# Latent attention and ternary gated experts: query weights in four held transfers, two transposes in accumulator banks

## The chip, the cores and the metric

The kernel runs on one core of one Trainium2 chip. The metric is the device time of one execution in microseconds, the lower the better. The core has TensorE (PE: matrix products and transposes into PSUM banks), VectorE (DVE), ScalarE (ACT), GpSimd (POOL) and SyncE (SP), whose queue issues every transfer between the chip's memory and the on-chip memory. The engines run side by side and wait for one another by semaphores.

## The reference

The input is a batch of 2 sequences of 2048 rows of 512 numbers, 4096 rows in all. Two layers follow one another, each with a layer norm ahead, a layer norm behind and a residual addition:

```python
Q = (hidden_states @ Wq.T + bq).reshape(b, t, H, HD).transpose(0, 2, 1, 3)
V = (hidden_states @ Wv.T + bv).reshape(b, t, H, HD).transpose(0, 2, 1, 3)
attn_logits = jnp.einsum('bhtd,lhd->bhtl', Q, latent) / math.sqrt(HD)
topk_logits, topk_idx = jax.lax.top_k(attn_logits, K_TOP)
attn_weights = jax.nn.softmax(topk_logits, axis=-1)
weighted = jnp.einsum('bhtk,bhtkd->bhtd', attn_weights, selected)
attn_output = (weighted + V).transpose(0, 2, 1, 3).reshape(b, t, d)
return attn_output @ Wo.T + bo
...
scale = jnp.mean(jnp.abs(w)) + EPS
q = jnp.clip(jnp.round(w / scale), -1.0, 1.0) * scale
hidden = jax.nn.silu(up) * gate
return jnp.einsum('bse,de->bsd', hidden, wd)
...
x = x + _layernorm(_L0_attn_ref(_layernorm(x, axis=-1), ...))
x = x + _layernorm(_L0_ffn_ref(_layernorm(x, axis=-1), ...))
```

There are 16 heads of 32 numbers, 64 latent keys for each head, of which a row keeps the best 4, and 2048 hidden units in the experts, whose three weight matrices are reduced to the signs -1, 0 and 1 times one scale each.

## The kernel before

The 4096 rows are worked in 8 blocks of 512 rows, a block in 4 tiles of 128 rows. For a block, the attention part normalizes the rows, brings them into the transposed form (512 features on the partitions), projects queries (4 chunks `c` of 128 features, each a sum over 4 pieces `k` of the query weights), forms the logits with the latent keys, finds the best four on VectorE, and projects values and output. The expert part then runs over 16 chunks of 128 hidden units. In the steady state the attention of one block is woven into the expert loop of the block before.

The change lies in the start, ahead of the first expert loop. There the order of the work on all engines is the hand-written list `FIRST_STEPS`: each word is a step, looked up in the dictionary `STEPS`, with its numbers as arguments, and every engine carries out its instructions in the order in which the steps issue them. The words that matter here are:

- `ast t`: `a_stats` of tile t of the first block, two VectorE instructions (L249, L250).
- `ars lo_hi`: `a_rstd`, the reciprocal root for the tiles lo to hi - 1, two GpSimd instructions (L256, L257). The first one covers two tiles, the others one each.
- `aap t`: `a_apply`, the normalization of tile t on VectorE (L276).
- `atr t`: `a_trans_pe`, four TensorE transposes of a tile into one PSUM bank (L286). The bank comes from `at_psum`, a pool of two buffers that everything short-lived uses.
- `acp t`: `a_copy`, the copy of that bank into the transposed rows `hT`, on ScalarE (L571) but for tile 3, which VectorE copies (L569).
- `q c`, `qc c`: the four products of query chunk c (L577) in a bank of `acc_psum`, a pool of four buffers, and its copy with the bias on ScalarE (L592). The first needs all four tiles of `hT`.
- `hold`: `hold_weights`, which writes one column of the latent keys' tile `lk` on VectorE (L853) and then issues the transfers of `load_weights` on SyncE. The transfer of `lk` has to wait for that write, and in SyncE's order all later ones stay behind it.
- `bh`, `bl`: preparation of the output bias, on ScalarE and VectorE; `nst`: statistics of the second block; `l`, `lc`: logits and their copy (L602, L610); `m`, `r`, `e`, `n`: the best four and the softmax (VectorE and ScalarE, L385 to L413); `s` with u, g or d and a number: the sum of absolute values of one piece of up, gate or down weights on ScalarE (L206); `totg`: the total over the gate pieces on TensorE (L214).

Ahead of the list SyncE issues the four row tiles of the first block (`load_x(0)`, L134) and the query weights as a single transfer of 1 MB (L161). TensorE meanwhile runs 16 products of a matrix of ones (L187), whose results nobody reads; each is two passes in the trace. `load_weights` then issues the latent keys, the biases, the value weights (1 MB), the latent values, the output bias, the second block's rows, and the up, gate, output and down weights in a fixed order. Transfers use eight semaphores in turn, so a transfer is issued only when the eighth before it has landed.

Of the kernel before, what the change touches and what calls it, by code (L numbers as in the profile page):

```python
# [17 lines left out]
P = 128  # L18
# [14 lines left out]


FIRST_STEPS = """
ast0 hold ast1 ars0_2 ast2 ars2_3 ast3 ars3_4 aap0 aap1 atr0 aap2 atr1 acp0 aap3 atr2 acp1 atr3 acp2 acp3 q0 bh
q1 qc0 bl nst0 l0 nst3 qc1 su0 nst1 v0 lc0 nst2 lc1 nrs su2 m1 su3 m0 l1 su1 r0 q2 lc2 su5 nap0
e0 r1 su6 ntr0 qc2 q3 ncp0 nap3 su7 nap1 nap2 sg1 n0 sg2 ob0 ob1 m2 ob2 e1 v1 qc3 n1 lc3 sg4 r2
t0 t1 tc0 ob3 tc1 sg5 m3 ntr2 e2 ntr1 ncp2 r3 y0 ncp1 l2 yc0 sg7 o3_0 n2 e3 o2_0 sd0 n3 v3 lc5
# [19 lines left out]
def latent_attention_ternary_glu(  # L59
# [15 lines left out]
    nc = tc.nc  # L75
    NT, D = x_in.shape
    E = wuT.shape[1]
    DC = D // P
# [18 lines left out]
    def at_psum(name):  # L97
        return ps_at.tile([P, 512], F32, tag="at", name=name)
# [11 lines left out]
    def transposed(which, b, name, dtype):  # L110
        return work.tile([P, DC, TB], dtype, tag=f"{which}{b % 2}", name=name, bufs=1)
# [17 lines left out]
    def load_x(b):  # L129
        x_tiles[b] = []  # L130
        for t in range(TT):
            xt = work.tile([P, D], F32, tag="x", name=f"x_{b}_{t}", bufs=2 * TT)
            r = b * TB + t * P
            nc.sync.dma_start(out=xt, in_=x_in[r : r + P, :])  # L134
            x_tiles[b].append(xt)
# [10 lines left out]
    def load_up(n, src, pieces):  # L146
        for i in pieces:
            k, h = halves[i]
            nc.sync.dma_start(
                out=raw[n, i], in_=src[k * P : (k + 1) * P, h * CH : (h + 1) * CH]  # L150
            )

    load_x(0)
    wq = wpool.tile([P, DC, D], F32, name="wq")
# [3 lines left out]
    bo_sb = wpool.tile([P, D], F32, name="bo_sb")  # L158
    lk = wpool.tile([P, DC, 2 * L], F32, name="lk")
    lv = wpool.tile([P, H // 2, HP], F32, name="lv")  # L160
    nc.sync.dma_start(out=wq, in_=wqT.rearrange("(c p) n -> p c n", p=P))  # L161

    def load_weights():
        nc.sync.dma_start(out=lk, in_=latk)
        nc.sync.dma_start(out=bqv_sb, in_=bqv)
        nc.sync.dma_start(out=wv, in_=wvT.rearrange("(c p) n -> p c n", p=P))
        nc.sync.dma_start(out=lv, in_=latv)
        nc.sync.dma_start(out=bo_sb, in_=bo.to_broadcast([P, D]))
        load_x(1)
        load_up("u", wuT, (0, 2, 3, 1, 5, 6, 7, 4))  # L170
        load_up("g", wgT, (1, 2, 4, 5))
        nc.sync.dma_start(out=wo, in_=woT.rearrange("(c p) n -> p c n", p=P))
        load_up("g", wgT, (7, 6, 0, 3))
        for i in (0, 2, 3, 6, 7, 9, 8, 1, 5, 4):
            rows = 2 * P if i < 6 else P
            r = i * 2 * P if i < 6 else 12 * P + (i - 6) * P
            nc.sync.dma_start(
                out=raw["d", i].rearrange("p (c n) -> p c n", n=D),
                in_=wdT[r : r + rows, :].rearrange("(c p) n -> p c n", p=P),
            )  # L180
# [2 lines left out]
    both = work.tile([P, 2, P], F32, tag="hid", name="ones", bufs=2)  # L183
    ones = both[:, 0, :]
    nc.vector.memset(ones, 1.0)
    for i in range(16):
        nc.tensor.matmul(at_psum(f"ones_{i}")[:, :P], lhsT=ones, rhs=ones, start=True, stop=True)  # L187
    ident = wpool.tile([P, P], F32, name="ident")
    make_identity(nc, ident)
# [93 lines left out]
    def transpose_row(h, name, psum=at_psum):  # L283
        pt = psum(f"pt_{name}")
        for c in range(DC):
            nc.tensor.transpose(pt[:, c * P : (c + 1) * P], h[:, c * P : (c + 1) * P], ident)  # L286
        return pt.rearrange("p (c k) -> p c k", k=P)
# [252 lines left out]
    class FirstAttention(Attention):  # L540
# [19 lines left out]
        def a_trans_pe(self, t):  # L560
            if self.hT is None:
                self.hT = transposed("X", self.b, f"hT_{self.b}", F32)
            self.pt = getattr(self, "pt", {})
            self.pt[t] = transpose_row(self.rows.pop(("a", t)), f"a{self.b}_{t}")

        def a_copy(self, t):
            dst, src = self.hT[:, :, t * P : (t + 1) * P], self.pt.pop(t)
            if self.b == 0 and t == 3:
                nc.vector.tensor_copy(dst, src)  # L569
            else:  # L570
                nc.scalar.copy(dst, src)  # L571
# [277 lines left out]
        return work.tile([P, TB], F32, tag=tag, name=f"qT_0_{c}", bufs=2)  # L849


    def hold_weights():
        nc.vector.memset(lk[:, 0, 0:1], 0.0)  # L853
        load_weights()

    STEPS = {
        "ast": A.a_stats,
# [6 lines left out]
        "l": A.l_pe,  # L864
        "lc": A.l_copy,
        "hold": hold_weights,
        "m": A.m,
        "r": A.r,
# [296 lines left out]
```

## Time and profile before

| what | us |
|---|---|
| median of 4 runs | 1142.31 |
| lowest and highest run | 1141.56, 1142.65 |
| the profiled execution, its own time | 1142.39 |
| its span, first to last instruction | 1140.6 |
| VectorE busy in it | 835.6 |
| ScalarE busy in it | 412.5 |
| the query weights' transfer: issue at, time to landing | 2.57, 7.9 |
| a piece of up weights (512 KB), issue to landing, median of 8 | 8.0 |
| TensorE waiting for rows of tile 0 (L286) | 0.80 |

Times within the profile count from the first instruction. A line of an instruction group gives the line of the kernel, the engine, the operation, the tile written and the tiles read, their shapes, how often it ran, how long it was busy, and the idle time of its engine just before it with the instruction or transfer that ended it. Products on TensorE overlap, so two of them lie closer together than one is long. "Issue to landing" of a transfer contains the time in which it stands behind others.

### The profile page before, as it was taken

What the parts mean: (1) busy time and instruction counts of PE and PEld (TensorE: products, weight loads), DVE (VectorE), ACT (ScalarE), POOL (GpSimd) and SP (SyncE); (2) the same over time, 40 slices, a digit from 0 to 9 for tenths busy, and PEclk for the clock granted to TensorE, in tenths of its full rate; (3) what the DMA queues carried; (4) which work ended last, traced back from release to release, by engine and by line L of the source; (5) the groups of instructions that cost most, each with busy time, mean ns of one, the idle gap of its engine ahead of it and who ended that gap; (6) DMA issues with size and microseconds to landing.
All of it is one profiled execution on the core that took longest, in us unless ns stands there. A gap on an engine that the chain in (4) does not pass through costs nothing.

```text
span 1140.6 us, 14491 instructions
## 1 busy us (share of the span) xinstructions
PE 1127.6 (99%) x4602; PEld 771.7 (68%) x4602; DVE 835.6 (73%) x2952; ACT 412.5 (36%) x715; POOL 164.7 (14%) x204
## 2 busy tenths in 40 slices
PE   8999999999999999999999999999999999999997
PEld 5547666767667665766667766586675866758885
DVE  6978968687866887678877778678786787846435
ACT  4985542332233332333214333153322433224223
POOL 1057003110032000320002200022001120020100
PEclk9999999999999999999999999999999999999999
DMA  9800221432213322222222223242321412102001
GB/s 346 309 0 22 72 93 42 107 120 84 85 50 97 102 87 79 73 76 93 93 74 75 83 93 97 61 102 64 117 71 56 111 65 93 63 3 74 37 1 37
DMA packets 98572, 97.16 MB, mean 85 GB/s; under 512 B 8384, under 2 KB 71104, under 8 KB 98496
## 3 DMA queue, kind: packets, MB, share of 16 engines
q1 hardware_dynamic: 98496, 96.24, 27.2%
q8 instruction: 36, 0.59, 0.2%
q14 instruction: 40, 0.33, 0.1%
HBM read 59.51 MB, written 36.70 MB: 84 GB/s over the span
## 4 chain that ended last, share of the span: by engine, by line
PE 87%; DMA 6%; DVE 5%; ACT 1%; issue 0%; SPq 0%; DVEq 0%; ACTq 0%
PE pg L716 19%; PE pu L716 19%; PE acc L759 18%; PE po L468 8%; PE pv L440 8%; PE pq L353 7%; PE pv L457 2%; PE pl L367 2%; DMA hT<-far_a 2%; DMA raw_d<-in_wdT 1%; DVE left L393 1%; DMA raw_g<-in_wgT 1%; DMA wv<-in_wvT 1%; DVE m L385 1%; PE pq L577 1%; DMA raw_u<-in_wuT 1%
## 5 line engine op out<-in xcount | busy, mean ns | idle before, releaser
L716 PE MATMUL pg<-hT_f,tern_g 128*128 128x512 f32 x512 | 207.8, 406 | 0.0
L716 PE MATMUL pu<-hT_f,tern_u 128*128 128x512 f32 x512 | 204.9, 401 | 0.0
L759 PE MATMUL acc<-tern_d,hi 128*128 128x512 f32 x512 | 203.6, 398 | 0.0
L759 PE MATMUL acc<-tern_d,lo 128*128 128x512 f32 x512 | 200.0, 391 | 1.0 <-DVE lo L749 0.8
L716 PE MATMUL pg<-lT_f,tern_g 128*128 128x512 f32 x512 | 199.8, 390 | 0.0
L716 PE MATMUL pu<-lT_f,tern_u 128*128 128x512 f32 x512 | 199.1, 390 | 0.0
L725 ACT ACTIVATE h<-pu,columns 128x512 f32<-128x512 f32 x128 | 87.1, 681 | 203.0 <-PE pu L716 203.0
L728 DVE SCALAR_TENSOR_TENSOR h<-h,pu 128x512 f32<-128x512 f32 x128 | 85.9, 671 | 94.1 <-ACT h L725 94.1
L744 ACT CAST hi<-h 128x512 fp32r<-128x512 f32 x128 | 79.1, 618 | 199.0 <-DVE h L733 199.0
L733 DVE TENSOR_TENSOR h<-h,pg 128x512 f32<-128x512 f32 x128 | 86.5, 676 | 63.4 <-PE pg L716 62.2
L759 PEld LDWEIGHTS acc<-tern_d,hi 128*128 128x128 f32 x512 | 96.1, 188 | 32.9 <-issue 13.6
L716 PEld LDWEIGHTS pg<-hT_f,tern_g 128*128 128x128 f32 x512 | 96.1, 188 | 25.3 <-issue 1.4
L716 PEld LDWEIGHTS pu<-hT_f,tern_u 128*128 128x128 f32 x512 | 96.0, 188 | 25.2 <-issue 3.1
L759 PEld LDWEIGHTS acc<-tern_d,lo 128*128 128x128 f32 x512 | 96.2, 188 | 22.8 <-DVE lo L749 2.2
L716 PEld LDWEIGHTS pu<-lT_f,tern_u 128*128 128x128 f32 x512 | 96.2, 188 | 22.5 <-issue 3.1
L716 PEld LDWEIGHTS pg<-lT_f,tern_g 128*128 128x128 f32 x512 | 96.3, 188 | 21.5 <-issue 2.9
L749 DVE TENSOR_TENSOR lo<-h,hi 128x512 fp32r<-128x512 f32 x128 | 89.8, 702 | 23.2 <-ACT hi L744 23.2
L440 PE MATMUL pv<-hT,wv 128*128 128x512 f32 x224 | 100.7, 593 | 0.4 <-ACT w L375 0.4
L393 DVE MATCH_REPLACE8 left<-m,w 128x64 f32<-128x64 f32 x512 | 100.3, 208 | 0.0
L468 PE MATMUL po<-wo,attnT 128*128 128x512 f32 x224 | 97.3, 592 | 0.0
L353 PE MATMUL pq<-hT,wq 128*128 128x512 f32 x192 | 86.8, 595 | 1.2 <-DMA hT<-far_a 1.0
L468 PEld LDWEIGHTS po<-wo,attnT 128*128 128x128 f32 x224 | 42.6, 190 | 50.7 <-issue 48.5
(141 smaller groups left out, 1312.4 us busy)
## 6 DMA issues: line engine op xcount, KB each, us to landing
dz<-z SPq DMA_DIRECT2D x56, 256.0 KB, 2.0
wT<-dz SPq DMA_DIRECT2D x224, 64.0 KB, 2.0
x<-in_x SPq DMA_DIRECT2D x32, 256.0 KB, 3.5
out_x<-x SPq DMA_DIRECT2D x31, 256.0 KB, 2.0
far_f<-zf SPq DMA_DIRECT2D x28, 256.0 KB, 2.8
hw<-far_f SPq DMA_DIRECT2D x56, 128.0 KB, 3.5
xa<-in_x SPq DMA_DIRECT2D x6, 1024.0 KB, 5.5
far_a<-za SPq DMA_DIRECT2D x24, 256.0 KB, 2.9
```

Source lines behind the costliest of these rows:

```text
L353: nc.tensor.matmul(pq, lhsT=wq[:, k, c * P : (c + 1) * P], rhs=self.taken(k), start=(k == 0), stop=(k == DC - 1),)
L367: nc.tensor.matmul(pls[pr][:, t * P : (t + 1) * P], lhsT=qT[rows, t * P : (t + 1) * P], rhs=lk[rows, c, :], start=True, stop=True, tile_po ...
L393: nc.vector.match_replace(left[:, g, :], m8[:, g, :], w[:, g, :], TAKEN)
L440: nc.tensor.matmul(self.pv[c], lhsT=wv[:, k, c * P : (c + 1) * P], rhs=self.ordered(k), start=(k == 0), stop=False,)
L468: nc.tensor.matmul(self.po[t], lhsT=self.attnT[:, c, t * P : (t + 1) * P], rhs=wo[:, c, :], start=(c == 0), stop=(c == DC - 1),)
L716: nc.tensor.matmul(p, lhsT=tern[n, 2 * k + e // 8][:, (e % 8) * P : (e % 8 + 1) * P], rhs=self.parts[i][:, k], start=(k, i) == pairs[0], s ...
L725: nc.scalar.activation(self.h[e], self.pu[e], AF.Tanh, scale=half_u[0])
L728: nc.vector.scalar_tensor_tensor(self.h[e], self.h[e], 1.0, self.pu.pop(e), ALU.add, ALU.mult)
L733: nc.vector.tensor_tensor(self.h[e], self.h[e], self.pg.pop(e), ALU.mult)
L744: nc.scalar.copy(hi, self.h[e])
L749: nc.vector.tensor_tensor(lo, self.h.pop(e), self.hid[e][0].bitcast(F32), ALU.subtract)
L759: nc.tensor.matmul(self.acc[t], lhsT=part[:, t * P : (t + 1) * P], rhs=wd, start=(e == 0 and i == 0), stop=(e == EC - 1 and i == 1),)
```

## The change

The query weights become four transfers of 256 KB, one for each piece `k`, and are no longer issued directly behind the rows: a first hold, placed behind the statistics of tile 0, writes one column of `wq` on VectorE and then issues them. A second hold, behind the statistics of tile 2, does the same with `lk` and issues all other weights, which were held behind tile 0 before. The matrix of ones is multiplied 20 times, not 16. The transposes of tiles 2 and 3 of the first block go into banks of the accumulator pool, and of these tiles VectorE copies tile 2 and ScalarE tile 3, the reverse of before.

```diff
-ast0 hold ast1 ars0_2 ast2 ars2_3 ast3 ars3_4 aap0 aap1 atr0 aap2 atr1 acp0 aap3 atr2 acp1 atr3 acp2 acp3 q0 bh
+ast0 hold0 ast1 ars0_2 ast2 hold1 ars2_3 ast3 ars3_4 aap0 aap1 atr0 aap2 atr1 acp0 aap3 atr2 acp1 atr3 acp2 acp3 q0 bh
...
-    nc.sync.dma_start(out=wq, in_=wqT.rearrange("(c p) n -> p c n", p=P))
-
-    def load_weights():
+    def load_weights(group):
+        if group == 0:
+            for k in range(DC):
+                nc.sync.dma_start(out=wq[:, k, :], in_=wqT[k * P : (k + 1) * P, :])
+            return
         nc.sync.dma_start(out=lk, in_=latk)
...
-    for i in range(16):
+    for i in range(20):
         nc.tensor.matmul(at_psum(f"ones_{i}")[:, :P], lhsT=ones, rhs=ones, start=True, stop=True)
...
-            self.pt[t] = transpose_row(self.rows.pop(("a", t)), f"a{self.b}_{t}")
+            psum = acc_psum if self.b == 0 and t >= 2 else at_psum
+            self.pt[t] = transpose_row(self.rows.pop(("a", t)), f"a{self.b}_{t}", psum)
...
-            if self.b == 0 and t == 3:
+            if self.b == 0 and t == 2:
                 nc.vector.tensor_copy(dst, src)
...
-    def hold_weights():
-        nc.vector.memset(lk[:, 0, 0:1], 0.0)
-        load_weights()
+    def hold_weights(group):
+        nc.vector.memset((lk if group else wq)[:, 0, 0:1], 0.0)
+        load_weights(group)
```

## The prediction

> **What bounds the kernel now.** I read the busy shares first, then the chain of waits over the first 60 us, then the timeline of the first 16 us, then busy time in half-microsecond stretches, and last ScalarE and VectorE around 43 us, where the chain turns from a transfer to an engine.
>
> ```profile
> PE 1127.6 (99%) x4602; PEld 771.7 (68%) x4602; DVE 835.6 (73%) x2952; ACT 412.5 (36%) x715; POOL 164.7 (14%) x204
> ```
>
> TensorE is idle for 1140.6 - 1127.6 = 13 us in all, so a change of the start is worth at most some of that, and the diff touches nothing behind the start. The timeline (start, us; engine, line, operation; idle before and what ended it):
>
> ```profile
> 1.03 6.76 PE L187 MATMUL ones<-ones 128*128 128x128 f32 x32 [1.03 <-DVE ones L185]
> ...
> 3.42 0.69 DVE L249 BATCH_NORM_STATS2 st_a<-x 128x6 f32<-128x512 f32 x1 [2.44 <-DMA x<-in_x]
> ...
> 6.31 0.70 DVE L249 BATCH_NORM_STATS2 st_a<-x 128x6 f32<-128x512 f32 x1 [1.15 <-DMA x<-in_x]
> ...
> 7.93 2.04 DVE L276 TENSOR_SCALAR h_a<-x,mv_a,rs_a 128x512 f32<-128x512 f32 x4
> ...
> 8.58 0.81 POOL L257 TENSOR_TENSOR rs_a<-rs_a,minus_half 128x1 f32<-128x1 f32 x1
> 8.60 1.08 PE L286 MATMUL pt_a<-ident,h_a 128*128 128x128 f32 x8 [0.80 <-DVE h_a L276]
> ...
> 9.90 1.15 PE L286 MATMUL pt_a<-ident,h_a 128*128 128x128 f32 x8 [0.22 <-ACT hT L571]
> ...
> 11.08 0.69 DVE L569 COPY hT<-pt_a 128x512 f32<-128x512 f32 x1 [1.10 <-PE pt_a L286]
> ...
> 11.87 4.53 PE L577 MATMUL pq<-hT,wq 128*128 128x512 f32 x10 [0.83 <-ACT ones L648]
> ```
>
> The first projection starts at 11.87, after: third row tile lands (6.31), its statistics, POOL's two reciprocal roots (8.58 + 0.81 = 9.39), fourth tile normalized (9.43 to 9.98), its transposes, its copy (to 11.77). Transposes three and four also wait for a bank (9.90). What the transfers did meanwhile (busy per engine, clock, DMA share, GB/s):
>
> ```profile
> 4.00:4.50 0.50, 0.50 (x4) 0.50 (x4) 0.47 (x4) 0.00 (x0) 0.00 (x0) 1.00 0.95 340
> 4.50:5.00 0.50, 0.50 (x4) 0.50 (x4) 0.47 (x2) 0.00 (x0) 0.00 (x0) 1.00 1.41 254
> 5.00:5.50 0.50, 0.50 (x5) 0.50 (x4) 0.16 (x1) 0.00 (x0) 0.19 (x1) 1.00 1.82 57
> 5.50:6.00 0.50, 0.50 (x4) 0.50 (x4) 0.00 (x0) 0.00 (x0) 0.47 (x1) 1.00 0.28 98
> ```
>
> There is a lull: bytes nearly stop between 5 and 6 us, when the last rows and the first query weights are in flight together. That is why tile three lands at 6.3 rather than about 4.7. But an earlier projection is not yet an earlier end. Two more views, the chain and then ScalarE and VectorE there:
>
> ```profile
> 5.50 8.46 DMA wv<-in_wvT
> ...
> 31.77 11.73 DMA raw_d<-in_wdT
> ...
> 45.24 1.13 DVE m L385 x8
> ```
>
> ```profile
> 43.58 1.06 ACT L206 ACTIVATE junk<-raw_d 128x1024 bf16<-128x1024 f32 x1 [0.70 <-DMA raw_d<-in_wdT]
> ...
> 45.24 0.86 DVE L385 MAX8 m<-w 128x8 f32<-128x64 f32 x6 [0.67 <-ACT w L610]
> ```
>
> The weights stream at 402 GB/s (mean of 15 to 45 us). The first down-weight piece lands at 43.5, ScalarE has waited 0.70 us for it, the copy queued behind it comes late, and VectorE waits 0.67 us. The waits of VectorE list no other from 21.75 to 67.4, where its work ends; then ScalarE's sums release TensorE at 69.15, and from there everything is relative. So **two gates meet at 45.24**: VectorE, ready at 44.58, and the weight stream. With D the gain of the stream and G that of the first projection, the end moves by the smaller of D and G + 0.67.
>
> **The change, part by part.**
>
> *Rows alone in the queue.* Tile one lands 2.7 us after its issue (0.72 to 3.40). At the 389 GB/s that the queue reaches at 3 us, 256 KB take 0.67, so the tiles land at 3.40, 4.07, 4.75 and 5.42. VectorE's step per tile is 0.83 (6.31 to 7.14): statistics at 3.42, 4.25, 5.08, 5.91; the added memset costs 0.06 (row L853); first normalization at 5.91 + 0.06 + 0.79 = 6.76, not 7.93. POOL's two single roots, 7.31 to 9.39 = 2.08 us, start when its first pair is done (6.25), so end at 8.35; tile four is normalized from 8.39 to 8.94, 1.04 earlier. Bounds: nothing (the lull comes anyway) and 1.04.
>
> *Banks and copies.* Transposes three and four lose their wait (0.22 on TensorE). The last copy goes to ScalarE: 0.59 instead of VectorE's 0.69. The copy of tile three on VectorE is done before tile four's. The accumulator rotation is displaced by two tiles of four buffers; each allocation still follows the fourth before it, and the other pair also still alternates (20 and 16 are both even), so no later wait is added.
>
> *Four more warm-ups.* Each is two passes. The 32 passes run from 1.03; the early ones are 0.213 apart (seven in 1.70, of which the last one's length is 0.42). The last six, from 6.74, take 1.05, of which the last one's length is 0.28; with one early step among the five, the others are 0.14. TensorE is free at 7.63 and then waited 0.80 for a normalized row. Eight more passes cost 0.9 (at the transposes' 0.11), 1.1 (at 0.14) or 1.7 (at 0.213). I take 1.1: free at 8.73. **They use up the cover**: the first row is now ready at 7.3, so the warm-ups, not the rows, release the transposes. Four tiles at 0.46 each (8.60 to 9.06): 8.75, 9.21, 9.67, 10.13; last pass 0.35 later; copy 0.31 after that, 10.79; 0.59 long; 0.10 to the projection: 11.48. **G = 0.4.** Ends: at 0.213 a pass, 12.1 (G = -0.2); if the warm-ups run faster earlier and only the rows bind, 8.94 + 0.15 + 0.35 + 0.31 + 0.59 + 0.10 = 10.44 (G = 1.4).
>
> The Trainium skill, page "TensorE: Matmul & The Clock Gate", Part 1, says the clock opens after one full busy window of about 3.4 us that runs freely against the kernel. This trace agrees as far as one run can: the spacing halves at 6.96, 5.9 us after the first pass. By the rule it could as well be anywhere from 3.4 to 6.8 us after it, which puts the warm-ups' end at 7.6 to 8.9 and G at 0.2 to 1.4.
>
> *Held query weights.* SyncE issues them after the memset, at 4.37, and 0.47 apart (x rows), so 4.37, 4.84, 5.31, 5.78. Queued behind them on SyncE: the other weights, formerly from 4.37 on, now from 6.25, which is also after the second memset (5.9). Landing: by the row tiles' 2.7, at 7.1 to 8.5; by the old single transfer's 7.9, at 12.3 to 13.7. The first piece is wanted at 11.48, the fourth six passes of 0.43 later, 14.06. So only the first piece could hold the projection, 0.8 at the worst end. By bytes: rows done at 5.42, 1 MB more at 389 GB/s, 8.1. I take that, since the old 7.9 contain the lull and a megabyte of rows ahead.
>
> The page "DMA: Bandwidth & Descriptors", Rules for kernel authors, speaks against it: at least 1 MiB per transfer for bandwidth, some 2 us fixed cost for each. Taken one after the other, four would cost 4 x 2.6 = 10.4 us, an estimate from that page, and the stream would be late by some 7.7. The two first row tiles disagree: issued 0.44 apart, they take 2.7 and 2.8 to land, so fixed parts overlap.
>
> *The stream, D.* From 4.5 to 7.5 the six half-microseconds moved 254, 57, 98, 238, 238 and 319 GB/s; against 406 that is 616 KB, 1.5 us. By landing of the query weights, 10.47 before and 8.1 now, it is 2.4. If the lull returns in full behind the hold, 0. The bytes of the held weights can start 1.0 after issue (rows: 0.72 to 1.7), 5.4, just as the rows end: no hole. I take 1.2, the middle.
>
> **Sum**: smaller of 1.2 and 0.4 + 0.67 = 1.07: 1.1 us. The profiled execution took 1142.39 (span 1140.6, 1.8 around it), 0.08 above the median of the four runs, so: 1142.3 - 1.1 = **1141.2**.
>
> **The rivals.**
>
> *A: nothing comes through.* The lull is no matter of the query weights; it strikes rows or weights again. Then D is 0, raw_d lands at 43.5 as before, and whatever G is, it ends in VectorE's wait at 45: 1142.3. For: from 7.5 to 50 us the stream stays near 400 GB/s though transfers of many tensors meet there, so their meeting alone is no cause. Against: it sets in just where the two meet.
>
> *B: both relieved in full.* D = 2.4, G = 1.4: smaller of 2.4 and 2.07, so 2.1: 1140.2. For: the rows alone allow 10.44. Against: the warm-ups' spacing in this trace.
>
> *C: slower.* One mechanism: the query pieces stay in the queue as long as 256 KB pieces do in the stream (lv 8.4, bo 8.2): the fourth lands at 5.78 + 8.3 = 14.1, against 10.47; the stream is 3.6 late, VectorE's gate goes from 45.24 to 48.9: 1145.9. It costs from a landing after 10.5, and over 0.2% from 12.8. Against: those rows stand behind up to 2 MB, these behind 1.
>
> **How the numbers follow.** Forecast 0.42, A 0.18, B 0.27, C 0.13. A difference of 0.2%, 2.3 us, is about what a measurement of this kernel can tell from none. Below 1140.0: with runs spread by half a microsecond each way, somewhat over half of B (0.16) and the edge of the forecast (0.04): 0.20. Above 1144.6: most of C (0.11) and 0.02 for what I overlook: 0.13. The rest, 0.67, is no difference. Range 1139.7 to 1143.6: it holds forecast, A, most of B, and C's mild part.
>
> **What would show it.** Third row tile's statistics at 5.1, tile four normalized by 9.0, no bank wait at 9.9, the first projection near 11.5, released by the last copy; TensorE without a hole between warm-ups and transposes. Query pieces landed by 8.5; ScalarE's wait at 43.5 shorter or gone and VectorE's `m` near 44.1. I am wrong if GB/s fall below 100 again behind 5 us (A), if the transposes start before 8 (B), or if the first projection is released by a transfer (C).

## The result and the profile after

The changed kernel takes 1143.45 us (median of 33 runs, 1142.71 to 1145.79), the kernel before 1142.24 (median of 53): a ratio of 1.0013, 95% interval 1.0008 to 1.0017. It is **slower by 0.9 to 1.9 us**; the forecast was 1.1 faster. The profiled execution took 1143.82 with a span of 1141.9, 1.3 longer than the span before.

Busy shares of the changed kernel: TensorE has 0.6 us more work (eight more passes of ones) and 0.7 us more idle time.

```profile
PE 1128.2 (99%) x4610; PEld 771.7 (68%) x4610; DVE 835.2 (73%) x2953; ACT 412.6 (36%) x715; POOL 164.8 (14%) x204
```

The timeline of its start (start, duration, engine, line, operation, idle before):

```profile
1.03 6.86 PE L189 MATMUL ones<-ones 128*128 128x128 f32 x40 [1.03 <-DVE ones L187]
...
4.39 1.75 SPq L164 DMA_DIRECT2D wq<-in_wqT  x4
...
5.93 0.69 DVE L251 BATCH_NORM_STATS2 st_a<-x 128x6 f32<-128x512 f32 x1 [0.74 <-DMA x<-in_x]
...
6.89 0.33 SPq L166 DMA_DIRECT2D lk<-in_latk  x1
...
7.59 2.04 DVE L278 TENSOR_SCALAR h_a<-x,mv_a,rs_a 128x512 f32<-128x512 f32 x4
...
8.25 2.10 PE L288 MATMUL pt_a<-ident,h_a 128*128 128x128 f32 x16 [0.35 <-DVE h_a L278]
...
10.38 0.59 ACT L574 COPY hT<-pt_a 128x512 f32<-128x512 f32 x1 [0.39 <-PE pt_a L288]
...
11.02 7.13 PE L580 MATMUL pq<-hT,wq 128*128 128x512 f32 x16 [0.68 <-ACT hT L574]
```

The first projection starts at 11.02, 0.85 earlier than before, and the transposes run as one group of 16 with no wait for a bank inside. But SyncE issues the query weights at 4.39 instead of 2.57 and the latent keys, with everything behind them, at 6.89 instead of 4.37. What that does to the transfers is in the table of stretches (last three columns: granted clock, DMA share, GB/s). The changed kernel:

```profile
5.00:5.50 0.50, 0.50 (x6) 0.50 (x4) 0.18 (x1) 0.00 (x0) 0.19 (x1) 1.00 0.47 168
5.50:6.00 0.50, 0.50 (x6) 0.47 (x5) 0.07 (x1) 0.00 (x0) 0.45 (x1) 1.00 1.12 238
...
7.00:9.00 2.00, 1.65 (x15) 1.42 (x14) 1.97 (x5) 0.09 (x1) 1.75 (x4) 1.00 0.90 272
9.00:12.00 3.00, 2.32 (x15) 1.46 (x13) 1.25 (x3) 1.77 (x4) 0.05 (x1) 1.00 0.80 256
12.00:16.00 4.00, 4.00 (x11) 1.85 (x10) 0.00 (x0) 0.00 (x0) 0.00 (x0) 1.00 0.96 330
16.00:44.00 28.00, 25.85 (x117) 13.43 (x116) 24.39 (x134) 23.47 (x47) 1.21 (x2) 1.00 1.03 402
```

The same stretches of the kernel before:

```profile
7.00:9.00 2.00, 1.20 (x10) 1.02 (x9) 1.93 (x7) 0.00 (x0) 1.44 (x4) 1.00 1.01 385
9.00:12.00 3.00, 1.95 (x16) 1.42 (x14) 1.59 (x3) 1.86 (x4) 0.39 (x1) 1.00 1.06 391
12.00:16.00 4.00, 4.00 (x10) 1.85 (x11) 0.00 (x0) 0.61 (x2) 0.00 (x0) 1.00 1.05 377
16.00:44.00 28.00, 27.50 (x120) 14.22 (x120) 26.47 (x139) 23.56 (x48) 1.21 (x2) 1.00 1.03 404
```

The lull at 5 to 6 us is partly filled (168 and 238 GB/s where it was 57 and 98), and the same stretch is paid for behind it. From 7 to 16 us the changed kernel moves 2 x 113 + 3 x 135 + 4 x 47 = 819 KB less; from 4 to 7 it had moved 222 KB more. The net 597 KB are 1.5 us at 403 GB/s, and from 16 us on both kernels run at one rate, so the loss is never made up. The first down piece lands at 44.99 instead of 43.49, that much later. These are two single profiles. The lull of the kernel before is largely one profile's: in the run with only banks and warm-ups further down, whose transfers are those of before, the same two half-microseconds carry 242 and 274 GB/s, more than in the changed kernel.

The chain of waits of the changed kernel (start, duration, what) shows where it reaches the engines:

```profile
5.24 5.27 DMA wq<-in_wqT
...
13.00 8.77 DMA raw_u<-in_wuT
21.78 1.15 ACT junk L208 x2
...
23.94 1.12 DVE m L387 x8
...
46.76 1.10 DVE m L387 x8
```

The chain runs through the first **up** piece (`raw_u`), the sum over it on ScalarE (`su0`), the logit copy that stands behind this sum, and from 23.94 on through VectorE without a break. ScalarE and VectorE there in the changed kernel:

```profile
21.78 1.06 ACT L208 ACTIVATE junk<-raw_u 128x1024 bf16<-128x1024 f32 x1 [2.19 <-DMA raw_u<-in_wuT]
...
22.84 1.06 ACT L613 ACTIVATE w<-pl 128x512 f32<-128x512 f32 x2
...
23.94 1.11 DVE L387 MAX8 m<-w 128x8 f32<-128x64 f32 x8 [0.27 <-ACT w L613]
```

And before:

```profile
19.02 0.69 ACT L592 ACTIVATE qT<-pq,bqv_sb 128x512 f32<-128x512 f32 x1 [2.42 <-PE pq L577]
...
19.60 1.05 ACT L206 ACTIVATE junk<-raw_u 128x1024 bf16<-128x1024 f32 x1
...
21.75 1.11 DVE L385 MAX8 m<-w 128x8 f32<-128x64 f32 x8 [0.50 <-ACT w L610]
```

Before, the sum started right behind the projection's copy; its piece had landed at 19.30, 0.3 us in time. Now ScalarE waits 2.19 us for it, and VectorE begins its best four 2.19 later (23.94 against 21.75). Before, VectorE had 0.67 us to spare at 45.24; 2.19 - 0.67 = 1.52 is what the end loses by this gate in this profile. (In the three variants with both holds the up piece lands at 20.12 to 20.36, and there the down piece alone sets the end; the table further down has them.) The gate of before, the first down piece, stands at the same place still, though the chain doesn't show it. Here ScalarE and VectorE of the changed kernel:

```profile
45.07 1.06 ACT L208 ACTIVATE junk<-raw_d 128x1024 bf16<-128x1024 f32 x1 [0.76 <-DMA raw_d<-in_wdT]
...
46.73 1.11 DVE L387 MAX8 m<-w 128x8 f32<-128x64 f32 x8
```

ScalarE waits 0.76 us for the down piece (0.70 before), and VectorE comes to its `m` at 46.73 without idle time, just when the copy behind the sum is done. Either gate alone would put the end 1.5 later: 46.73 instead of 45.24, and the total over the gate pieces at 70.65 instead of 69.15.

### The profile page after: what moved, and what is told of

The parts are those of the page before. It is cut to its first block, busy times and chain, and to the rows that moved or that the text cites. A ratio compares the mean times of both kernels' runs of the same rounds, so it can differ in the third digit from the quotient of the medians.

```text
span 1141.9 us, 14510 instructions
## 1 busy us (share of the span) xinstructions
PE 1128.2 (99%) x4610; PEld 771.7 (68%) x4610; DVE 835.2 (73%) x2953; ACT 412.6 (36%) x715; POOL 164.8 (14%) x204
## 4 chain that ended last, share of the span: by engine, by line
PE 88%; DVE 6%; DMA 2%; ACT 1%; SPq 1%; issue 1%; DVEq 0%; ACTq 0%
PE pg L719 20%; PE pu L719 19%; PE acc L762 19%; PE po L470 8%; PE pv L442 8%; PE pq L355 7%; PE pv L459 2%; PE pl L369 2%; DVE left L395 2%; DVE m L387 1%; DMA hT<-far_a 1%; DMA raw_u<-in_wuT 1%; DVE w L397 1%; DVE w L415 1%; PE pq L580 1%
```

## The experiments

My theory was that the holds cost the transfers time and the rest of the change gains or is neutral. Rivals: the split into four pieces keeps them long in the queue (C); the warm-ups or the banks cost; the hold does serve the rows. The runs of one group share their runs of the kernel before.

**One query transfer in place of four**, both holds kept:

```diff
-            for k in range(DC):
-                nc.sync.dma_start(out=wq[:, k, :], in_=wqT[k * P : (k + 1) * P, :])
+            nc.sync.dma_start(out=wq, in_=wqT.rearrange("(c p) n -> p c n", p=P))
```

> The changed kernel, but the query weights are one held transfer of 1 MB again. Theory 'pieces' (four pieces of 256 KB fill four of the eight transfer slots or are read more slowly): 9 to 14 us carry 380 GB/s or more as before, the first up piece lands near 20 and the time falls to 1142.3 or below. Rival 'second hold' (the other weights are issued 2.5 us later): nothing changes, 1143.4, the first up piece still lands after 21.

Measured: 1143.1, ratio 1.0009 (1.0000 to 1.0018). Still on the slow side; the down piece lands at 44.28 and 9 to 12 us carry 306 GB/s, as theory 'pieces' would not have it. The first up piece does land near 20, at 20.12. The split isn't what makes the kernel slow; whether it adds a little, these intervals don't tell.

**The second hold directly behind the first:**

```diff
-ast0 hold0 ast1 ars0_2 ast2 hold1 ars2_3 ast3 ...
+ast0 hold0 hold1 ast1 ars0_2 ast2 ars2_3 ast3 ...
```

> The changed kernel with the second hold directly behind the first, so that the latent keys and all other weights are issued right behind the query pieces, near 6.2 us and not 6.9. Theory 'second hold': stream earlier by up to 0.7 us, time 1142.7 or below. Rival 'pieces': the stream stays near 270 GB/s from 9 to 14 us and the time within 0.3 of 1143.4.

Measured: 1142.65, 1.0005 (0.9996 to 1.0014); up piece 20.33, down piece 44.42. The time is what theory 'second hold' asked for, but the interval reaches from no loss to the whole of it, and the landings are those of the run with only the transfers below, which has both holds in their places (20.36 and 44.43). So a gain of the earlier second hold isn't shown.

**Only banks and warm-ups** (transfers as before):

```diff
-    for i in range(16):
+    for i in range(20):
...
+            psum = acc_psum if self.b == 0 and t >= 2 else at_psum
...
-            if self.b == 0 and t == 3:
+            if self.b == 0 and t == 2:
```

> The kernel before with only the accumulator banks, the exchanged copies and the 20 products of ones; its transfers are untouched. Theory 'the whole loss is in the stream': no loss, the time within 0.4 of 1142.2, the first projection between 11.4 and 11.9. Rival 'the banks or the warm-ups cost': 1142.8 or more.

Measured: 1142.39, 1.0004 (0.9995 to 1.0013). No loss that the interval shows, and the up piece lands at 19.63, the down piece at 42.86 with the transfers as they were. Its stretches at the lull:

```profile
5.00:5.50 0.50, 0.50 (x5) 0.50 (x4) 0.18 (x1) 0.00 (x0) 0.19 (x1) 1.00 0.95 242
5.50:6.00 0.50, 0.50 (x4) 0.50 (x4) 0.19 (x1) 0.00 (x0) 0.42 (x1) 1.00 1.07 274
```

**Only the transfers** (split and holds; 16 warm-ups, transposes and copies as before):

> The changed kernel with 16 products of ones, banks and copies as before: only the two holds and the four query pieces remain. Theory 'the whole loss is in the stream': 1143.4 or a little more. Rival 'the banks or the warm-ups cost': 1142.8 or less.

Measured: 1142.93, 1.0005 (0.9996 to 1.0014); up piece 20.36, down piece 44.43. The time lies between the two expectations. The loss sits in the transfers: the interval alone would not show it; the landings do (42.86 to 43.49 for the down piece where the transfers are those of before).

**Four pieces, not held.** The kernel before with only this:

```diff
-    nc.sync.dma_start(out=wq, in_=wqT.rearrange("(c p) n -> p c n", p=P))
+    for k in range(DC):
+        nc.sync.dma_start(out=wq[:, k, :], in_=wqT[k * P : (k + 1) * P, :])
```

> The kernel before with the query weights in four transfers, issued directly behind the rows as the single one was; the hold for the rest is where it was. Theory 'pieces': the first down piece lands over 0.8 us later than before's 43.5 (the unchanged transfers of the banks run: 42.9), time 1143 or more. Rival 'late issue' (the loss comes from issuing the query weights at 4.4 rather than 2.6): it lands within 0.5 of 43.2, time within 0.4 of 1142.2.

Measured: 1141.35, 0.9993 (0.9984 to 1.0002), span 1139.1. The stretches of this run, columns as above:

```profile
5.00:5.50 0.50, 0.50 (x5) 0.50 (x4) 0.19 (x2) 0.00 (x0) 0.18 (x1) 1.00 0.64 225
5.50:6.00 0.50, 0.50 (x5) 0.50 (x4) 0.46 (x1) 0.00 (x0) 0.42 (x2) 1.00 0.98 332
...
7.00:9.00 2.00, 1.42 (x11) 0.97 (x10) 1.90 (x6) 0.52 (x2) 1.46 (x3) 1.00 1.02 376
9.00:12.00 3.00, 2.05 (x10) 1.32 (x11) 0.90 (x2) 1.34 (x4) 0.00 (x0) 1.00 1.06 398
```

At the place of the lull the stream is fuller than with the holds (225 and 332), and nothing is lost behind it. The down piece lands at 42.06, earlier than either side expected; the first projection starts at 11.10.

**One query transfer, held; the rest directly behind it:**

```diff
-    nc.sync.dma_start(out=wq, in_=wqT.rearrange("(c p) n -> p c n", p=P))
...
     def load_weights():
+        nc.sync.dma_start(out=wq, in_=wqT.rearrange("(c p) n -> p c n", p=P))
...
-        nc.vector.memset(lk[:, 0, 0:1], 0.0)
+        nc.vector.memset(wq[:, 0, 0:1], 0.0)
```

> The kernel before with the single query transfer moved behind the memset that follows the first rows' statistics, and all other weights directly behind it: one hold, one transfer. Theory 'late issue': the stream is late by up to the 1.8 us of the later issue, the first down piece lands at 44.2 or later, time 1142.9 or more. Rival 'pieces': it lands within 0.5 of 43.2.

Measured: 1143.4, 1.0011 (1.0003 to 1.0020). Its stretches from 5.5 to 12 us:

```profile
5.50:6.00 0.50, 0.50 (x4) 0.50 (x4) 0.31 (x1) 0.00 (x0) 0.43 (x1) 1.00 1.23 160
6.00:7.00 1.00, 1.00 (x7) 1.00 (x6) 0.97 (x3) 0.00 (x0) 0.51 (x3) 1.00 0.40 117
7.00:9.00 2.00, 1.91 (x14) 1.50 (x13) 1.89 (x6) 0.36 (x1) 1.61 (x3) 1.00 0.85 319
9.00:12.00 3.00, 1.69 (x10) 1.13 (x10) 1.05 (x2) 1.50 (x4) 0.00 (x0) 1.00 1.00 322
```

The first hold by itself opens a hole from 6 to 7 us: 117 GB/s where the kernel before moves 238. The lull of the kernel before evens that out (154 GB/s from 5 to 7 us against its 158). The loss lies behind: 319 and 322 GB/s where the kernel before moves 385 and 391. The down piece lands at 44.63, as theory 'late issue' had it.

**The second hold alone** (query weights as before):

```diff
-ast0 hold ast1 ars0_2 ast2 ars2_3 ast3 ...
+ast0 ast1 ars0_2 ast2 hold ars2_3 ast3 ...
```

> The kernel before with its hold for the other weights moved from the first to the third rows' statistics (from 4.4 to about 7 us); the query weights stay one transfer, not held. Theory 'late issue': the single megabyte ahead covers most of the wait, the first down piece lands at 43.5 to 44.2, time 1142.2 to 1142.9. Rival 'second hold': 44.2 or later, 1143 or more. If neither moves, only query weights issued late do harm.

Measured: 1143.7, 1.0012 (1.0003 to 1.0021). Here the loss comes late:

```profile
7.00:9.00 2.00, 1.39 (x11) 0.95 (x10) 1.89 (x6) 0.41 (x1) 1.56 (x3) 1.00 1.00 371
9.00:12.00 3.00, 1.95 (x11) 1.32 (x11) 1.00 (x2) 1.44 (x4) 0.00 (x0) 1.00 0.88 292
12.00:16.00 4.00, 4.00 (x11) 1.71 (x10) 0.00 (x0) 0.00 (x0) 0.00 (x0) 1.00 1.03 310
```

The query weights cover the first hole, up to 9 us; from 9 to 16 the stream runs at 292 and 310 instead of 391 and 377. The down piece lands at 45.53, later than theory 'late issue' allowed, as the rival had it: the megabyte ahead doesn't cover the wait. By the intervals, the cost of either hold alone can't be told from that of both together.

**A down sum behind the logit copies** (kernel before; does ScalarE's wait at 43.5 set the end?):

```diff
-... o2_0 sd0 n3 v3 lc5
-lc4 m5 sd2 ...
+... o2_0 n3 v3 lc5
+lc4 m5 sd0 sd2 ...
```

> The kernel before with ScalarE's first sum over down weights moved behind the two logit copies it kept waiting (and behind the best-four of one of them). If the gate is what the prediction took it for, VectorE starts that best-four at 44.6 and not 45.2, the total over the gate weights comes at 68.5 and not 69.15, the time falls by 0.6 to 1141.6. Rival 'the chain only looks like that': the total stays at 69.1 within 0.2.

Measured: 1141.93, 1.0001 (0.9991 to 1.0010). ScalarE and VectorE at the place:

```profile
42.30 1.10 ACT L610 ACTIVATE w<-pl 128x512 f32<-128x512 f32 x2
...
43.25 1.09 ACT L206 ACTIVATE junk<-raw_d 128x1024 bf16<-128x1024 f32 x1
...
44.58 1.10 DVE L385 MAX8 m<-w 128x8 f32<-128x64 f32 x8
```

The copies no longer wait for the down piece, and VectorE's `m` starts at 44.58, the very time at which the prediction has VectorE ready. The total over the gate weights comes at 68.49, as expected. The gate is real, but not all of the 0.66 is the order's: the down piece also lands earlier in this profile (43.05), and with the old order the rule of the next section gives 44.80. The span gains 0.3, and the times can't tell it from nothing.

**The changed kernel without its holds** (four pieces behind the rows, the rest held behind tile 0 as before; 20 ones, banks and copies kept):

> The changed kernel without its two holds: four query transfers directly behind the rows, the single hold for the rest where it was, 20 products of ones, the banks and the exchanged copies. Theory 'the holds are the whole loss': first down piece by 42.5, total over the gate weights by 68.2, time 1141.2 to 1141.7. Rival 'holds and something else of the change (the 20 products, the banks)': 1142.2 or more.

Measured: 1141.8, 0.9997 (0.9988 to 1.0006); the down piece lands at 42.79, 2.2 earlier than with the holds, the total comes at 68.47. All three are just later than theory had them, and the interval lies wholly below the changed kernel's (1.0008 to 1.0017). So the new places of the two transfer groups account for the loss.

**Rows with nothing behind them in the queue:**

```diff
-ast0 hold0 ast1 ars0_2 ast2 hold1 ars2_3 ast3 ars3_4 ...
+ast0 ast1 ars0_2 ast2 ars2_3 ast3 hold0 hold1 ars3_4 ...
```

> The changed kernel with both holds behind the fourth tile's statistics: nothing is issued behind the rows until they are done. The prediction's 'the query weights in the queue delay the rows' would land tile three near 4.75 and tile four near 5.4. Rival 'the rows stall by themselves': 5.3 to 5.9 and 6.0 to 6.6 as in all kernels so far. Either way, if the holds cost by their lateness (query weights from 4.4 to about 7), the first down piece lands at 46 or later and the time is 1144.5 or more.

Measured: 1146.48, 1.0034 (1.0022 to 1.0047). One instruction of its timeline, then its stretches:

```profile
5.80 0.69 DVE L251 BATCH_NORM_STATS2 st_a<-x 128x6 f32<-128x512 f32 x1 [0.65 <-DMA x<-in_x]
```

```profile
4.50:5.00 0.50, 0.50 (x4) 0.50 (x4) 0.47 (x2) 0.00 (x0) 0.00 (x0) 1.00 0.91 352
5.00:5.50 0.50, 0.50 (x5) 0.50 (x4) 0.15 (x1) 0.00 (x0) 0.19 (x1) 1.00 0.32 119
5.50:6.00 0.50, 0.50 (x4) 0.50 (x4) 0.20 (x1) 0.00 (x0) 0.48 (x1) 1.00 0.14 53
6.00:7.00 1.00, 1.00 (x9) 0.97 (x8) 0.97 (x3) 0.00 (x0) 0.43 (x2) 1.00 0.00 0
```

With no other transfer in the queue the third row tile is still not there before 5.78, and the queue runs dry. The trace keeps sixteen updates of a semaphore for each transfer, one for each share, the last of which is the landing: fourteen of the third tile's come by 4.98, two at 5.76 and 5.78. It is the rows' own last shares that come late, not the query weights that hinder them: in the seven other runs with query weights directly behind the rows the tile lands between 5.15 and 5.84. So a hold buys nothing on the rows. The down piece lands at 47.85: the more the weights are held, the more is lost.

**Pieces, banks and both sums moved.** On top of the unheld pieces and the banks (16 ones), `su0` and `sd0` go behind the logit copies that they held up:

```diff
-... qc1 su0 nst1 v0 lc0 nst2 lc1 nrs su2 ...
+... qc1 nst1 v0 lc0 nst2 lc1 su0 nrs su2 ...
...
-... o2_0 sd0 n3 v3 lc5
-lc4 m5 sd2 ...
+... o2_0 n3 v3 lc5
+lc4 m5 sd0 sd2 ...
```

> Four query transfers without a hold, the banks with 16 products of ones, and ScalarE's first up sum behind the first two logit copies and first down sum behind the last two. If the stream's two gates and nothing else bind, VectorE's first best-four starts near 20.1 instead of 21.0, the total comes near 67.0, time 1140.6. If TensorE itself binds there, the total stays at 67.4 or later, time 1141.0 or more.

Measured: **1140.33, 0.9983 (0.9974 to 0.9992)**, faster than both kernels. Its ScalarE and VectorE at the first gate, and the total over the gate pieces:

```profile
19.03 1.09 ACT L612 ACTIVATE w<-pl 128x512 f32<-128x512 f32 x2 [0.40 <-PE pl L604]
...
20.00 1.06 ACT L207 ACTIVATE junk<-raw_u 128x1024 bf16<-128x1024 f32 x1
...
20.15 1.11 DVE L386 MAX8 m<-w 128x8 f32<-128x64 f32 x8 [0.20 <-ACT w L612]
...
67.58 0.39 PE L215 MATMUL tot_g<-sums_g,ones 128*128 128x8 f32 x2
```

The logit copy waits for its product alone, and VectorE starts 1.6 us earlier than before; that much arrives at the total (69.15 to 67.58). The moved sums are not the whole of it: the four pieces alone, not held, have the total at 67.77 in their profile, and no run moves both sums without the pieces. The total is also later than the 67.0 expected of the stream alone; it is where the other expectation had it (67.4 or later, with TensorE binding), while the time is below both.

**The same without the banks:**

> As the run with pieces, banks and order, but transposes and copies as before. Theory 'TensorE has 1 us to spare here': within 0.2 of that run. Rival 'the banks matter once the stream does not bind': 0.2 to 0.4 later in the total over the gate weights.

Measured: 1140.96, 0.9986 (0.9977 to 0.9995). The banks add nothing that these intervals show. The total comes 0.31 later (67.89), as the rival had it, but in this profile the first up piece too lands later, at 19.10 instead of 18.06.

## Why the prediction was wrong

The step that failed is the stream's gain D. The prediction took it at +1.2, with nothing as its lower end, because the held weights would start just as the rows end and run at the queue's full rate. The runs show a loss in its place: with both holds the first down piece lands at 44.28 to 44.99, with the transfers of before at 42.86 to 43.49. That the time lies inside the stated range, 1139.7 to 1143.6, is luck: its upper part was there for a mild form of rival C, whose reason, the size of the pieces, is not the cause.

The frame of the prediction, an end set by the later of two gates, holds once a third is added. In every run that keeps ScalarE's order, the best four of chunk 0 start at the later of the first projection + 9.88 and the first up piece's landing + 2.18, and those of chunk 5 at the later of that + 22.79 and the first down piece's landing + 1.75. The constants are from the traces of before (21.75 - 11.87 = 9.88 and 45.24 - 43.49 = 1.75) and after (23.94 - 21.76 = 2.18 and 46.73 - 23.94 = 22.79); the other nine rows test them. Landings are read from the traces, in us, one profile for each row:

| run | first projection | up piece lands | down piece lands | chunk 5 by the rule | measured | span |
|---|---|---|---|---|---|---|
| before | 11.87 | 19.30 | 43.49 | 45.24 | 45.24 | 1140.6 |
| after | 11.02 | 21.76 | 44.99 | 46.74 | 46.73 | 1141.9 |
| one query transfer | 11.46 | 20.12 | 44.28 | 46.03 | 46.03 | 1141.5 |
| second hold early | 10.97 | 20.33 | 44.42 | 46.17 | 46.17 | 1141.6 |
| banks and ones | 11.29 | 19.63 | 42.86 | 44.61 | 44.61 | 1140.1 |
| transfers only | 11.47 | 20.36 | 44.43 | 46.18 | 46.18 | 1141.1 |
| four pieces, not held | 11.10 | 18.32 | 42.06 | 43.81 | 43.81 | 1139.1 |
| one transfer, held | 11.52 | 20.77 | 44.63 | 46.38 | 46.38 | 1141.4 |
| second hold alone | 11.20 | 20.76 | 45.53 | 47.28 | 47.28 | 1141.9 |
| changed, no holds | 10.92 | 19.51 | 42.79 | 44.54 | 44.54 | 1140.0 |
| rows alone | 11.04 | 24.63 | 47.85 | 49.60 | 49.60 | 1144.9 |

Span less the measured column is 1094.6 to 1095.5 throughout: what these gates lose, the kernel loses, to within that spread.

- *Rows alone in the queue: wrong in its premise.* Tile three was to land at 4.75 and its statistics to start at 5.08; they start at 5.93, and at 5.80 with nothing else in the queue. The hold left tile three where it lands anyway; the profile of before, with 6.29, had caught it at its latest (5.15 to 5.91 in all others). The bound "nothing" held.
- *Banks and copies: right.* The wait of 0.22 is gone, and no later one came.
- *Four more warm-ups: right that they are cheap, wrong that they bind.* They were to end at 8.73 and release the transposes. The last one starts at 7.62 and ends at 7.89, and VectorE's first row releases the transposes at 8.25 (`0.35 <-DVE h_a`). The passes come closer together from 4.18 us instead of 6.96 (the granted clock reads 1.00 throughout), and over the profiles of all 14 kernels this moment lies anywhere from 4.18 to 7.17 with the first pass always at 1.03. The Trainium skill, page "TensorE: Matmul & The Clock Gate", Part 1, has the gate's window run freely against the kernel; this spread agrees. The earliest moment, 3.15 us after the first pass, is a little before the 3.4 that the prediction took as the least. G came out at 0.85, not 0.4, inside its ends.
- *Held query weights: the premise of D that failed.* "The bytes of the held weights can start 1.0 after issue, 5.4, just as the rows end: no hole." The rows do not end as one block: their last tile lands at 6.55, not at 5.42, and what is missing is not a hole at 5.4 but rate from 7 to 16 us. The four pieces land at 9.2 to 11.15, not by 8.1. The prediction took the rows' 2.7 us and a full rate of 389 GB/s for a queue that a hold had emptied; the rate from 7 to 12 was 256 to 272. Its rival C, at 14.1, was too high. (Of the two first row tiles the second takes 2.9 to land, 1.16 to 4.04; the prediction's 2.8 is the median of both.)
- *D: the wrong sign.* Taken at +1.2 with nothing as its lower end, it is -1.5 between the two profiles, and -0.8 to -2.1 over all with both holds against all with the transfers of before. The bounds left out that issuing the weights 1.8 and 2.5 us later could lose more than the lull gave back. The nearest rule of the Trainium skill, in "DMA: Bandwidth & Descriptors", Rules for kernel authors, is to issue a transfer early and wait for it late. These runs agree, with the loss above; the rule gives no price for issuing late. The prediction weighed another rule of that table, at least 1 MiB for each transfer, which the unheld pieces don't bear out: four of 256 KB have landed by 8.95 to 9.68 in four profiles where the single one of 1 MB lands at 10.24 to 10.48 in three. The 2 us of fixed cost that the prediction names beside it are not in that table; the page has them under "Anatomy of one DMA", for transfers that GpSimd issues, and here SyncE issues them.
- *The smaller of D and G + 0.67: right where its terms held, incomplete otherwise.* Four pieces not held have D = 43.49 - 42.06 = 1.43 and G + 0.67 = 0.77 + 0.67 = 1.44; the gate moved by 45.24 - 43.81 = 1.43. But "VectorE, ready at 44.58" was taken to follow the projection alone. It also follows the first up piece, which before had 0.3 us to spare (19.30 against ScalarE free at 19.6). With the weights late, G reached no one.

Of the rivals, A's reason ("the lull is no matter of the query weights") holds for the rows, but not its price, nothing. C had the sign but not the mechanism: it blamed the size of the pieces, and pieces that are not held lose nothing.

**What stays open** is why the stream is not merely late behind a hold but slow. From 7 to 12 us it moves 263 to 299 GB/s in the changed kernel and its three variants with both holds, 321 and 324 with either hold alone, and 353 to 391 in the seven kernels with the old hold. SyncE's issues don't tell it: the four of the second block's rows, which wait for landings, span 3.08 us in the changed kernel and 3.82 before. The semaphore updates show part of it. In the changed kernel fourteen of the first held piece's sixteen come by 6.96, the last two at 9.17 and 9.20; in the run with four pieces not held all sixteen come from 5.92 to 6.99. With the second hold alone fifteen of the first down piece's come by 43.62 and the last at 45.53. So a few shares fall behind and set the landing. The others come later too: the mean of the first down piece's sixteen is 42.50 to 43.53 with both holds, 41.56 to 41.83 with the transfers of before. What holds them up isn't shown. The first up piece loses 2.46 us in the changed kernel's profile, more than the stream's 1.5, but with the same transfers in the run with only the transfers it loses 1.06; the rest varies from profile to profile.

## What to carry to other kernels

Where a queue of transfers feeds the path at its full rate, expect a held issue to come back at the end unless something is shown to keep the queue full: holding the two groups by 1.8 and 2.5 us cost 1.5 at the first down piece, holding both by 5.0 cost 4.4. Test the gain side too, by emptying the queue altogether. And take a lull from more than one profile before it goes into a sum. An engine that carries out its work in order passes on every wait of the instruction ahead: a sum that nobody needs yet, ahead of a copy that all wait for, makes its transfer part of the critical path. When a gate shows 0.3 us of slack, it belongs in the sum as a term, not in the background.

## What the runs showed of the hardware

- The first rows' transfers have a tail of their own: in the run with nothing behind them the rate falls from 352 GB/s (4.5 to 5) to 119 and 53 before the third tile is complete at 5.78 and the fourth at 6.42.
- Four transfers of 256 KB issued directly behind the rows have all landed by 8.95 to 9.68 us in four profiles, a single one of 1 MB in the same place at 10.24 to 10.48 in three. At the first down piece little of that is left: 42.06 to 42.86 against 42.86 to 43.49. The times agree in direction (0.9993, 0.9984 to 1.0002) without proving it.
- The moment at which TensorE's passes come closer together moves by up to 3.0 us between kernels whose products of ones start at the same time.
